# A graph-network kernel on one core: the last layer regrouped, its lists kept on chip, and buffer waits by bytes

## The chip, the cores and the metric

The kernel runs on one core of one Trainium2 chip. The metric is the device time of one execution in microseconds (us). Five executions of the kernel before took 2224.06, 2224.08, 2226.6, 2227.36 and 2230.5 us; the median is 2226.6 us.

The core has five engines that matter here, each with its own in-order queue: PE multiplies matrices, DVE does elementwise work, ACT does functions such as exp and also copies and casts, POOL does elementwise work and issues the indirect transfers (gathers and scatters whose row numbers lie in a tile), and SP issues the plain transfers. An instruction starts when those before it on its engine have started their turn and its semaphores have the values it waits for. So a wait holds up everything behind it on the same engine.

## The reference

The input x is 8 batches x 2048 nodes x 64 features, and adj is a 2048 x 2048 matrix of zeros and ones with ones on the diagonal. Four layers follow each other, each of the form x + layer(relu(layernorm(x))):

- layer 0: hypergraph attention over 64 hyperedges, mixed with the product of adj (rows divided by their degree) and the features;
- layer 1: a Chebyshev convolution with three terms, and a weight matrix for each node, made from 16 embeddings;
- layer 2: three steps of message passing with adj;
- layer 3: graph attention.

Layer 3 is the one that is changed most:

```python
h = jnp.einsum('bni,io->bno', x, weight)
e = leaky_relu((h @ a[:D, 0])[:, :, None] + (h @ a[D:, 0])[:, None, :], 0.2)
e = adj[None, :, :] * e
h_prime = jnp.einsum('bij,bjd->bid', softmax(e, axis=-1), h)
```

Where adj is 0 the score is 0 and not minus infinity. So a node's result is a weighted sum over its few neighbours plus one common weight times the sum of all other nodes' features.

## The kernel before

**Layout.** Most layers hold x as four pairs q of two batches, so 128 partitions are 2 batches x 64 features, in chunks of 512 nodes. The product with adj goes through 16 row tiles of adj (`adj_t`, loaded by SP, cast by ACT at L295, multiplied by PE into `pp`). Nodes are sorted by degree early on; `orders` holds the sorted order, 16 tiles of 128 nodes.

**Who sets the order.** The kernel is written with pools and tiles. A scheduler puts the instructions of each engine in an order of its own, so the order in the file is not the order of issue, and it adds the semaphore waits. A pool is released at the end of its `with` block. A tile of a later pool that lies on the same bytes waits; before the change it waits for all users of the released pool.

**Neighbour lists** (`neighbours`, L1468). While layer 2's first steps run on PE, DVE finds for each sorted tile t from 1 to 15 the node numbers of at most NEAR[t] neighbours of each of its 128 nodes (20, 14, 12, 10, 9, 8, 8, 7, 6, 6, 5, 5, 4, 4, 3, together 121). At its end two DVE instructions make row numbers and a mask of them, and SP stores both (128 x 242 numbers) to DRAM.

**The last layer.** `Scores` (L1880 on) computes for each tile of nodes the 512 features of h (8 batches x 64) and 16 scores, and stores them as rows of 528 numbers in DRAM (`f_rows`). Then `layer3_near` (L1520) builds a `Near` object and runs two generators side by side:

- `first_tile` (L2039) handles tile 0, the 128 nodes with the most neighbours, densely. It gathers their rows of adj, transposes them (`at`), and goes through 16 column tiles jt. For each, DVE copies the features to `h` (L2092), which has a column of ones; PE adds the plain product (`plain`). For each of 8 batches ACT computes two exps (L2099, L2100), DVE takes their maximum (L2101) and multiplies it by adj (L2102), 128x128 each, and PE adds the product with h (`first`). It yields after each batch.
- `others` (L1987) handles the tiles 1 to 15 in the order TILES, one block each. `block` (L1970) has POOL gather the tile's own rows and those of its neighbours from f_rows into a ring of 40 rows (`fetch`, L1953; the gathers show as L1955). Some ten small DVE instructions and two exps on ACT make the weights (L1999 to L2016). Then DVE multiplies each gathered row by its weights (`scaled`, L2034, 128x512) into one of four buffers, the sum of all rows last, and PE adds it through the identity matrix into `acc`. It yields after each row. A division gives `o`. The block after the next one is then gathered, and `put_back` (L1964) has POOL scatter the `o` of the block before to DRAM (`att_rows`, L1966).

Each yield of `others` lets `first_tile` take one step. When both are done, `result` (L2122) loads `att_rows` in 16 tiles of 256 KB (L2132) into three buffers, PE transposes them (L2135), DVE adds them to x (L2137; x is loaded a chunk at a time into two buffers, L2128), and SP stores each chunk in four pieces (L2141).

**Other lines that the prediction touches.** L1264 and L1268 load the convolution's weights, L1271 subtracts two of them, and `pk` are its products; L1228 are transposes for layer 1; L607 is the end of layer 0's mixing; L203 makes the low half of a split number (`ah_n_lo` among them).

## Time and profile before

| | |
|---|---|
| median of five executions | 2226.6 us |
| the profiled execution | 2230.18 us |
| its span from the first to the last instruction | 2228.5 us |
| mean granted TensorE clock | 0.904 |
| instructions | 21758 |
| TensorE busy | 1959.0 us (88%) |
| VectorE busy | 1136.8 us (51%) |
| POOL busy | 708.2 us (32%) |
| data moved | 254.03 MB |

The span divides into layer 0 (0 to 680 us), layer 1 (680 to 1397), layer 2 (1397 to 1934) and the last layer (1934 to 2228). In the page's slices each digit is the busy share of a fortieth of the span, 55.7 us. In lists of groups, a row has the line, the engine, the operation, the tiles written and read, and the count; then busy time in us and the mean duration of one in ns; then the idle time of the engine just before such instructions and what ended it. In timelines a row has start and duration in us, and in brackets the idle time before it. DVE instructions overlap: the next one starts some 0.08 us before the end of the one before, so the time from start to start is shorter than the duration. POOL's gathers show 0.95 us or more each, with 0.30 us of issue between them.

### The profile page before, as it was taken

The numbers are of one execution on the slowest core, as the hardware profiler recorded it, in microseconds if no ns is written. First come the engines' busy times: TensorE is split into PE (matmuls) and PEld (weight loads), VectorE is DVE, ScalarE is ACT, GpSimd is POOL, SyncE is SP. The second block draws the span as 40 slices with busy tenths as digits, with TensorE's granted clock in tenths as the row PEclk, the third lists the DMA queues.
The fourth block names the chain that finished last, engine by engine and source line by source line (L and its number), as shares of the span: only waits on it lengthen the run. The fifth ranks groups of instructions, "written<-read, shape, count | busy, mean of one in ns | idle before, by whom it ended". The sixth has DMA issues, their size and how long they took to land.

```text
span 2228.5 us, 21758 instructions
## 1 busy us (share of the span) xinstructions
PE 1959.0 (88%) x7530; PEld 1191.7 (53%) x7530; DVE 1136.8 (51%) x2292; ACT 711.0 (32%) x1331; POOL 708.2 (32%) x609
## 2 busy tenths in 40 slices
PE   5777899997879998999999998998999999679883
PEld 1454766662226775344353543776777677445442
DVE  7846667754663121533425344897402222359892
ACT  6402355544443442011020200422534333245430
POOL 0013066755330001735727266012000000177740
PEclk8857799997676998999999999899999999789895
DMA  8231123352103345022050400455434444377735
GB/s 319 69 100 28 44 92 106 125 157 85 38 38 107 125 106 163 0 94 58 23 128 0 114 1 22 171 189 197 155 113 133 133 152 143 124 198 199 205 107 201
DMA packets 108032, 254.03 MB, mean 114 GB/s; under 512 B 19632, under 2 KB 20032, under 8 KB 100608
## 3 DMA queue, kind: packets, MB, share of 16 engines
q1 hardware_dynamic: 90288, 185.46, 26.4%
q0 software_dynamic: 17616, 67.00, 10.1%
q8 instruction: 63, 1.03, 0.2%
q14 instruction: 65, 0.53, 0.1%
HBM read 218.49 MB, written 33.93 MB: 113 GB/s over the span
## 4 chain that ended last, share of the span: by engine, by line
PE 59%; DVE 10%; POOL 5%; DMA 5%; issue 4%; ACT 3%; SPq 1%; POOLq 0%; DVEq 0%; ACTq 0%
PE pp L136 24%; PE pk L136 16%; PE acc L136 5%; PE bank L136 4%; PE p L136 2%; POOL ring L1955 2%; PE pn L136 2%; DMA q<-in_adj_dram,order 2%; POOL dt L633 1%; POOL q L1794 1%; DMA adj_t<-in_adjT_dram 1%; PE pd L136 1%; DVE q L1809 1%; DMA q<-att_rows 1%; PE pt L1228 1%
## 5 line engine op out<-in xcount | busy, mean ns | idle before, releaser
L295 ACT CAST adj<-adj_t 128x512 fp32r<-128x512 f32 x384 | 237.0, 620 | 728.9 <-PE pp L136 622.2
L1354 POOL TENSOR_TENSOR acc<-acc,y 128x512 f32<-128x512 f32 x224 | 277.1, 1269 | 450.1 <-DVE y L1349 450.1
L136 PE MATMUL pk<-q,w 128*128 128x512 f32 (+1 forms) x1024 | 358.3, 612 | 14.1 <-DVE w L1271 11.9
L136 PEld LDWEIGHTS pk<-q,w 128*128 128x128 f32 (+1 forms) x1024 | 136.6, 188 | 232.1 <-issue 181.2
L1349 DVE SCALAR_TENSOR_TENSOR y<-pk,bias,q 128x512 f32<-128x512 f32 x224 | 157.7, 746 | 139.8 <-PE pk L136 133.4
L136 PE MATMUL acc<-q,ident 128*128 128x512 f32 x416 | 218.3, 627 | 11.4 <-ACT q L1829 6.2
L136 PE MATMUL pp<-adj,u_n_hi 128*128 128x512 f32 x768 | 213.1, 397 | 0.0
L136 PE MATMUL pp<-adj,u_n_lo 128*128 128x512 f32 x768 | 209.2, 392 | 0.0
L136 PEld LDWEIGHTS pp<-adj,u_n_hi 128*128 128x128 f32 x768 | 143.9, 188 | 34.8 <-issue 6.4
L136 PEld LDWEIGHTS pp<-adj,u_n_lo 128*128 128x128 f32 x768 | 144.6, 188 | 29.6
L1955 POOL DMA_INDIRECT ring<-f_rows,near x121 | 124.6, 1030 | 36.9 <-issue 17.1
L2048 POOL IOTA q<- 128x2048 int32 x1 | 1.8, 1834 | 348.9 <-PE p L136 348.9
L1794 POOL TENSOR_TENSOR q<-q,beta 128x512 f32<-128x512 f32 x57 | 67.5, 1184 | 111.0 <-DVE pick L1750 79.6
L136 PEld LDWEIGHTS acc<-q,ident 128*128 128x128 f32 x416 | 73.2, 197 | 52.5 <-issue 26.6
L1349 DVE SCALAR_TENSOR_TENSOR acc<-pk,bias,q 128x512 f32<-128x512 f32 x32 | 22.6, 747 | 146.8 <-PE pk L136 146.8
L136 PE MATMUL pp<-adj,x_ind_hi 128*128 128x512 f32 x256 | 95.0, 488 | 2.2 <-DVE q L701 1.8
L2034 DVE TENSOR_TENSOR q<-ring,e 128x512 f32<-128x512 f32 x136 | 91.2, 683 | 3.5 <-PE acc L136 3.3
L136 PEld LDWEIGHTS first<-h,m 128*128 128x128 f32 x256 | 47.6, 203 | 78.8 <-DVE m L2102 35.3
L136 PE MATMUL bank<-std,from_rows 32*128 32x512 f32 x128 | 47.1, 911 | 41.9 <-DVE std L243 33.8
L136 PE MATMUL pp<-adj,h_n_hi 128*128 128x512 f32 x256 | 77.6, 415 | 0.0
L136 PE MATMUL pp<-adj,h_n_lo 128*128 128x512 f32 x256 | 75.4, 407 | 0.0
L136 PE MATMUL pp<-adj,ah_n_hi 128*128 128x512 f32 x256 | 73.7, 408 | 0.0
(381 smaller groups left out, 3238.7 us busy)
## 6 DMA issues: line engine op xcount, KB each, us to landing
adj_t<-in_adjT_dram SPq DMA_DIRECT2D x160, 512.0 KB, 3.8
rows<-in_adj_dram SPq DMA_DIRECT2D x16, 1024.0 KB, 5.4
adj_t<-in_adjT_dram SPq DMA_DIRECT2D x64, 256.0 KB, 3.1
q<-x SPq DMA_DIRECT2D x12, 1024.0 KB, 4.8
q<-in_embT_dram SPq DMA_DIRECT2D x8, 1024.0 KB, 11.4
x<-q SPq DMA_DIRECT2D x8, 1024.0 KB, 3.9
x_ch<-in_xT_dram SPq DMA_DIRECT2D x4, 1024.0 KB, 6.2
h_rows<-q SPq DMA_DIRECT2D x16, 256.0 KB, 2.9
```

The source lines that it names most:

```text
L136: self.nc.tensor.matmul(out, lhsT, rhs, start=start, stop=stop)
L295: nc.scalar.copy(moving, at[:, i])
L633: nc.gpsimd.tensor_sub(dt, th[0], th[1])
L1228: nc.tensor.transpose(pt[:, q], src(q)[h, s], ident[h, h])
L1349: nc.vector.scalar_tensor_tensor(y, pks[b, half], bias[:, b : b + 1], emb[:, b], op0=OP.add, op1=OP.mult,)
L1354: nc.gpsimd.tensor_add(acc, acc, y)
L1794: self.nc.gpsimd.tensor_tensor(x, x, by.unsqueeze(2).to_broadcast([P, NB, D]), op=OP.mult)
L1809: nc.vector.tensor_add(d, d, self.pas.pop(i - 1))
L1955: self.nc.gpsimd.indirect_dma_start(to, None, self.kern.f_rows[:], bass.IndirectOffsetOnAxis(ap=index, axis=0))
L2034: self.nc.vector.tensor_tensor(to.rearrange(split, b=NB), src.rearrange(split, b=NB), by.unsqueeze(2).to_broadcast([P, NB, D]), op=OP.mult,)
L2048: nc.gpsimd.iota(whole, pattern=[[1, N]], base=0, channel_multiplier=0)
```

## The change

Six things change.

1. Every pool is opened with `reuse_waits="tile"`: a tile on released bytes waits only for the users of these bytes, and no longer for all users of the released pool.
2. The neighbour lists stay on chip, in a tile that lives through the whole kernel (`kern.near`). The two DVE instructions that make row numbers and mask of them move from the end of `neighbours` to the start of the last layer; store and load go.
3. The ring has 36 rows instead of 40. The exps of `first_tile` get a tile of their own on a slot (`self.m`, two sets for all 8 batches); `result` gets 16 buffers for `att_rows` instead of three.
4. The start: gathers of the first two blocks are issued first, then `first_tile` takes twelve steps, then both go on side by side.
5. `others` multiplies two gathered rows with one DVE instruction of 128x1024, the sum of all rows and the first row first; it yields after two rows.
6. In `first_tile` ACT copies the features to `h`, of which there are two with fixed ones; max and multiplication take all 8 batches of a column tile in one DVE instruction of 128x1024; it yields four times per column tile.

```diff
-            tc.tile_pool(name="att", bufs=1) as w,
+            tc.tile_pool(reuse_waits="tile", name="att", bufs=1) as w,
...
-        near = k.tile([P, FIRST[NT]], F, name="near")
+        near = self.near
...
-        both = k.tile([P, 2, FIRST[NT]], I32, name="near_both")
-        nc.vector.tensor_scalar(both[:, 0], near, 1.0, -1.0, op0=OP.max, op1=OP.add)
-        nc.vector.tensor_scalar(both[:, 1].bitcast(F), near, 0.0, None, op0=OP.is_gt)
-        nc.sync.dma_start(self.near, both)
...
             near = Near(self, slots, w, ps)
             first = near.first_tile()
+            others = near.others()
             next(first)
-            for part in near.others():
+            next(others)
+            for _ in range(12):
+                next(first)
+            for part in others:
                 next(first, None)
...
-    RING = 40
+    RING = 36
...
+        self.m = slots.tile([P, 4, NB, P], F, name="m", tag="q0")
+        self.att = Halves(slots, "att", ("q0", "q1"), True)
...
-        near = w.tile([P, 2, FIRST[NT]], I32, name="near")
-        nc.sync.dma_start(near, kern.near)
-        self.near, self.there = near[:, 0], near[:, 1].bitcast(F)
+        self.near = w.tile([P, FIRST[NT]], I32, name="near")
+        nc.vector.tensor_scalar(self.near, kern.near, 1.0, -1.0, op0=OP.max, op1=OP.add)
+        self.there = w.tile([P, FIRST[NT]], F, name="there")
+        nc.vector.tensor_scalar(self.there, kern.near, 0.0, None, op0=OP.is_gt)
...
         ready = [self.block(t) for t in self.TILES[:2]]
+        yield
...
-            for i in range(n + 1):
-                y = self.y[:, self.turn % 4]
-                self.turn += 1
-                by, src = (e[:, i], block[:, i, : NB * D]) if i < n else (none, self.total)
-                self.scaled(y, src, by)
-                kern.mm(acc, kern.ident, y, start=i == 0, stop=i == n)
+            for i in range(-1, n, 2):
+                y = self.y[:, self.turn % 4 : self.turn % 4 + 2]
+                self.turn += 2
+                if i < 0:
+                    self.scaled(y[:, 0], self.total, none)
+                    self.scaled(y[:, 1], block[:, 0, : NB * D], e[:, 0])
+                elif i + 1 < n:
+                    nc.vector.tensor_tensor(
+                        y.rearrange("n i (b f) -> n i b f", b=NB),
+                        block[:, i : i + 2, : NB * D].rearrange("n i (b f) -> n i b f", b=NB),
+                        e[:, i : i + 2].unsqueeze(3).to_broadcast([P, 2, NB, D]), op=OP.mult,
+                    )
+                else:
+                    self.scaled(y[:, 0], block[:, i, : NB * D], e[:, i])
+                for j in range(min(2, n - i)):
+                    kern.mm(acc, kern.ident, y[:, j], start=i + j < 0, stop=i + j == n - 1)
                 yield
...
+        hs = [w.tile([P, NB, D + 1], F, name=f"h{i}") for i in range(2)]
+        for h in hs:
+            nc.vector.memset(h[:, :, D:], 1.0)
         for jt in range(NT):
-            h = w.tile([P, NB, D + 1], F, name="h", bufs=3)
-            nc.vector.memset(h[:, :, D:], 1.0)
-            nc.vector.tensor_copy(
-                h[:, :, :D], self.rows(jt).rearrange("n (b f) -> n b f", b=NB)
-            )
+            h = hs[jt % 2]
+            nc.scalar.copy(h[:, :, :D], self.rows(jt).rearrange("n (b f) -> n b f", b=NB))
+            m, m2 = (self.m[:, 2 * (jt % 2) + i] for i in range(2))
+            for b in range(NB):
+                nc.scalar.activation(m[:, b], on_all[:, 0, b], AF.Exp, bias=ed[:, jt, b : b + 1])
+                nc.scalar.activation(m2[:, b], on_all[:, 1, b], AF.Exp, bias=ed2[:, jt, b : b + 1])
+                if b % 4 == 3:
+                    yield
+            nc.vector.tensor_max(m, m, m2)
+            nc.vector.tensor_mul(m, m, at[:, jt].unsqueeze(1).to_broadcast([P, NB, P]))
+            yield
             kern.mm(plain, at[:, jt], self.rows(jt), start=jt == 0, stop=jt == NT - 1)
             for b in range(NB):
-                m = w.tile([P, P], F, name="m", bufs=4)
-                m2 = w.tile([P, P], F, name="m2", bufs=4)
-                nc.scalar.activation(m, on_all[:, 0, b], AF.Exp, bias=ed[:, jt, b : b + 1])
-                nc.scalar.activation(m2, on_all[:, 1, b], AF.Exp, bias=ed2[:, jt, b : b + 1])
-                nc.vector.tensor_max(m, m, m2)
-                nc.vector.tensor_mul(m, m, at[:, jt])
                 kern.mm(
-                    accs[b // 4][:, b % 4, : D + 1], m, h[:, b],
+                    accs[b // 4][:, b % 4, : D + 1], m[:, b], h[:, b],
                     start=jt == 0 and b % 4 == 0, stop=jt == NT - 1 and b % 4 == 3,
                 )
-                yield
+            yield
...
-                r = self.parts[:, t % 3]
+                r = self.att(t)
                 nc.sync.dma_start(r, kern.att_rows[t * P : (t + 1) * P])
```

## The prediction

> **What bounds the kernel.** I read the page's totals first, then the slices, then the last layer by itself. PE is busy for most of the span, and most of the change lies in the last layer, from 1934 us to the end:
>
> ```profile
> PE 1959.0 (88%) x7530; PEld 1191.7 (53%) x7530; DVE 1136.8 (51%) x2292; ACT 711.0 (32%) x1331; POOL 708.2 (32%) x609
> ...
> PE   5777899997879998999999998998999999679883
> ...
> DVE  7846667754663121533425344897402222359892
> ...
> POOL 0013066755330001735727266012000000177740
> ```
>
> Up to slice 34 PE follows PE, so there only PE's idle time can be won. In the last layer (slices 35 to 40) three engines are near their limits at once. The table of 10 us windows shows it (columns: window, length, PE, PEld, DVE, ACT, POOL busy, granted clock, DMA share, GB/s):
>
> ```profile
> 1990.00:2000.00 10.00, 1.20 (x3) 0.93 (x4) 3.07 (x13) 1.06 (x4) 7.56 (x9) 0.62 0.96 223
> ...
> 2040.00:2050.00 10.00, 10.00 (x34) 5.18 (x33) 10.00 (x30) 4.60 (x13) 7.87 (x8) 1.00 0.67 188
> ...
> 2150.00:2160.00 10.00, 7.18 (x21) 3.26 (x20) 9.73 (x28) 0.47 (x2) 2.41 (x2) 1.00 0.14 52
> ```
>
> POOL's 7.87 is a full queue: each gather shows 0.95 us of work and 0.30 us of issue. From 1939.07 to 2138 it starts 148 transfers without a pause, and nothing can end before its last gather, which starts at 2135.98. DVE and PE then still have four blocks to do; the last `o` is ready at 2176.2. So in the layer's first part the gathers set the time (1990 to 2000: everyone waits for the block of 21 rows), in the second part DVE with PE. The groups of this layer, by shape:
>
> ```profile
> L1955 POOL DMA_INDIRECT ring<-f_rows,near x121 | 124.6, 1030 | 36.9 <-issue 17.1 <-DVE m L2102 4.9 <-DVE m L2101 4.9
> L2034 DVE TENSOR_TENSOR q<-ring,e 128x512 f32<-128x512 f32 x136 | 91.2, 683 | 3.5 <-PE acc L136 3.3
> ...
> L2101 DVE TENSOR_TENSOR m<-m,m 128x128 f32<-128x128 f32 x128 | 36.2, 288 | 3.4 <-ACT m L2099 3.3
> L2102 DVE TENSOR_TENSOR m<-m,q 128x128 f32<-128x128 f32 x128 | 36.1, 286 | 0.0
> ```
>
> **What a DVE instruction does to a gather.** The releasers of L1955 are DVE lines, though no gather depends on them. The timeline shows why:
>
> ```profile
> 1945.32 0.95 POOL L1955 DMA_INDIRECT ring<-f_rows,order  x1 [0.30 <-issue]
> 1945.41 2.35 DVE L2052 SCALAR_TENSOR_TENSOR q<-q,own 128x2048 f32<-128x2048 int32 x1 [7.38 <-DMA q<-in_adj_dram,order]
> 1946.57 2.00 POOL L1955 DMA_INDIRECT ring<-f_rows,near  x1 [0.30 <-issue]
> ```
>
> The third line starts 1.16 us into a long two-input DVE instruction and takes 2.00 us instead of 0.95: it waited until that instruction was nearly through. Of the 110 transfers that start between 1991 and 2138, those that start inside a 128x512 L2034 are longer by up to 0.45 us, about what is left of it; the mean start-to-start time is 1.336 us instead of 1.25. The wait is thus 0.085 us per transfer. Random arrival would give 65 us of L2034 in 147 us times half of 0.60 us, 0.13, plus 0.03 for the short ones; so about half of random was paid.
>
> **Part 1, DVE's work in the last layer.** Instructions back to back start every 0.20 us (128x128) and 0.60 us (128x512), so an element of a row costs 1.04 ns and an instruction 0.07 us. A 128x1024 then takes 1.14 us. The nearest two-input row, L1271 at 64x1024, lasts 1.22 us against 0.683 for 512: bounds 1.14 and 1.37 (twice 512); I take 1.14. Behind the block of 21 rows there are 13.5 of 16 column tiles of the first tile and 53 of 58 pairs. Max and mul: 13.5 x (16 x 0.20 - 2 x 1.14) = 12.4 us; the copies to h that go to ACT, 13.5 x 0.41 = 5.5; pairs, 53 x (1.20 - 1.14) = 3. Together 21 us of the 154 us that DVE is busy from 2000 to 2170. ACT gets 16 copies of about 0.57 us and is busy 3 to 7 of every 10 us, so they cost nothing; if it were full they would cost 9 us. PE keeps its work: a row's two matmuls take 0.86 us at full clock and a head's 0.22. From 1997 on that is about 148 us, which by itself would end at 2145. Near lists from chip: two DVE instructions replace a 121 KB load (2.1 us) that the first gather waited for. The load of order stays in SP's queue, so the first gather starts about 1 us earlier (0 to 2). The ring of 36 only makes the last block wait for rows read long before: nothing, and at most one block's 5 us.
>
> So DVE's backlog behind the last gather shrinks to nothing, and **the gathers become the bound**. In the order of the changed program the last row is the 149th transfer from the first ring gather (146th before, two more scatters stand ahead). Its start is 1990.6 + 110 x (1.25 + w), w being the wait per transfer. Behind it come its landing, 4.5 us (a gather of 2067.40 lets its block start at 2072.44), and 13 us: the last block's scores stand ahead of six rows of the block before, so twelve rows at 0.86 and about 2.5 us of first multiply and `o`.
>
> Now w. Long two-input instructions, 53 pairs and 27 max or mul of 1.14 us, fill 91 us of about 155; a random arrival in one waits 0.57, so 0.34 in the mean. The lower bound is the 0.085 of today. I take 0.22, two thirds of random, nearest to the share paid today. Last gather 2152.3, last `o` 2169.8 against 2176.2: **-6 us**. With 0.085 it would be -20 (PE would then need 93% to follow), with 0.34 +7.
>
> The Trainium skill (SBUF — State Buffer, section "Who interferes with whom") says that a DVE instruction with two SBUF inputs contends with a GpSimd instruction that reads SBUF, and that the second to issue blocks fully. That speaks against longer instructions here. Taken at its word, every arrival waits, and this part would be +7 and the whole -10; the trace, with half of random, stands for less.
>
> **Part 2, the tail.** The chain after the last scatter:
>
> ```profile
> 2176.52 2.71 DMA att_rows<-o,order
> 2179.25 2.65 DMA q<-att_rows
> ...
> 2189.70 4.64 DMA q<-att_rows
> ...
> 2198.72 4.51 DMA q<-att_rows
> ...
> 2208.03 5.32 DMA q<-att_rows
> ```
>
> With three buffers, each set of loads waits for transposes, and SP issues it behind the stores of the chunk before. From 2179.25 the stores of the four chunks start 8.6, 17.1, 26.9 and 38.1 us later. Changed: nine loads go out at once, 0.45 us apart; a tile takes PE and DVE 1.02 us. Chunk 0 is done at 7.7 and chunk 1 at 11.8. The load of x for chunk 2 waits for the landing of chunk 0's stores (4.1 us after the last issue) and takes 5.0: 18.8. Chunk 2 is done at 22.6; the last two loads stand behind its stores in SP's queue, 24.4, land 4.6 later; chunk 3's stores start at 30. **-8 us**; -3 if the transfers only share what is already 0.97 and 0.88 busy in 2190 to 2210, -12 if they do not slow each other.
>
> **Part 3, waits at the seams.** I followed each buffer wait to the instruction that it names after the change. Four move where PE is idle. At 262.20 the first adjacency loads waited for the last reader of the released pool; their own bytes were free 5 us earlier; ACT waited 2.78 us for the landing and PE 4.55 behind it: -3 (0 to -3.5). At 76.6 the second phase's first product: -2 (0 to -2.6). At 675.7 transposes behind the last DVE of the mixing: -1 (0 to -2). At 828 the weight loads of the convolution:
>
> ```profile
> PE pk L136 <- DVE w L1271: 11.9, 1, 11.9
> ...
> DVE w L1271 <- DMA w<-in_wk_dram: 6.3, 1, 6.3
> ```
>
> SP is free to issue them from about 821 instead of 828.17. DVE is not done with ah_n_lo until 837.5, so at most 7 of the 11.9 us go; but the DMA share is about 1.0 from 822 on, so the loads may only move in among embT's: -3 (0 to -7). The other moved waits lie upstream of busy PE. **-9 us** (0 to -15). Everything behind a seam follows PE, so what is won is kept.
>
> **Sum.** -6 -8 -9 = -23 us on the profiled execution, 2230.2 (span 2228.5 and 1.7 around it): 2207. That execution lies 3.6 us above the median of the five, so 2204 for the median.
>
> **Rivals.** (a) The gathers keep their pace, w about 0.1, because scores and stalls leave gaps between the long instructions as today: part 1 is -19, the whole -36, 2191. For it: half of random today; against it: DVE's longest instruction doubles. (b) The waits at the seams are replaced by full DMA queues; parts 1 and 2 remain: -14, 2213. For it: the DMA share at 822. (c) Slower: a gather falls in step with PE's pace of a pair of rows, 1.72 us instead of 1.25. Then w is 0.47 through the layer, the last gather 2180, `o` 2197.7, 21.5 us later than before; with the other parts 2231, and 2240 if the seams give nothing. It is slower from w = 0.43 on. For it: 1.14 us is nearly one gather's cycle of 1.25, so a gather just released meets the next long instruction at its start. Against: where gathers are late, DVE idles and blocks nobody. (d) No change: w near 0.34 and a third of the seams and tail: within 0.2%, which is about what can be told from no change here.
>
> **Chances.** Forecast band 2195 to 2209, with its neighbours to 2218: 50%; (a) 18%; (b) up to 2222: 12%; (d) 8%; (c) 12%. Faster by over 0.2%: 80%. The range leaves out the far ends of (a) and (c): 2186 to 2229.
>
> **What would show it.** In the changed profile: the mean of the ring gathers near 1.17 us instead of 1.03 (near 1.05 would be rival a, 1.4 rival c), more of them released by DVE multiplies; DVE's busy time in the last layer down by 25 to 45 us, by count of instructions' durations; the wait for near gone; the chunk stores of the tail 30 us after its start; PE's wait for w near 9 us. I would be wrong most of all if DVE and PE lose time to each other on two pair buffers and lumps of eight heads, so that the backlog behind the last gather stays.

## The result, and the profile after

The changed kernel takes 2225.45 us (median of 42 runs) against 2228.41 us of the kernel before (79 runs): a ratio of 0.9985, 95% interval 0.9976 to 0.9994. The forecast was 2204. Only about a seventh of the forecast gain came; in the number the result is rival (d), no change within 0.2%, but not by that rival's account (below). The profiled execution has a span of 2224.3 us against 2228.5, at the same granted clock of 0.904.

Three places give the account. They are read from the two traces: how much earlier the n-th of the 7530 matmuls starts ("PE's lead"), the first gather into the ring, the end of the last `o`, and the end.

| | before | after | difference |
|---|---|---|---|
| PE's lead in the middle of layer 2 (1506 us) | | | -13.7 |
| PE's lead at the end of layer 2 (1922 us) | | | -6.3 |
| last matmul of the scores to first ring gather | 6.0 | 4.8 | -1.2 |
| first ring gather to last ring gather | 195.7 | 217.0 | +21.3 |
| last ring gather to last `o` | 40.3 | 26.8 | -13.4 |
| last `o` to the end | 52.2 | 47.9 | -4.3 |

So PE was 13.7 us ahead in the middle of layer 2, of which 7.4 were lost again inside layer 2, where the code is the same; the last layer's main part became 8 us longer instead of 6 shorter; the tail gave half of what was forecast.

The page of the changed kernel, its totals and slices:

```profile
PE 1967.1 (88%) x7530; PEld 1188.6 (53%) x7530; DVE 1116.5 (50%) x1980; ACT 708.9 (32%) x1347; POOL 727.9 (33%) x609
...
PE   5877899987879979999999998998999999679873
...
DVE  7846767744762032434424254998302222349763
...
POOL 0012066755420002726537176011000000277760
```

DVE has 312 instructions fewer, POOL as many as before but 20 us more of busy time. Ten-microsecond windows of the changed kernel (columns as in the windows above: length, PE, PEld, DVE, ACT, POOL, granted clock, DMA share, GB/s):

```profile
2040.00:2050.00 10.00, 9.08 (x32) 4.74 (x32) 9.96 (x16) 8.07 (x27) 7.87 (x8) 1.00 0.67 194
2120.00:2130.00 10.00, 4.02 (x6) 1.79 (x7) 4.81 (x14) 0.47 (x2) 7.69 (x8) 0.66 0.66 208
2140.00:2150.00 10.00, 6.55 (x8) 2.72 (x9) 6.23 (x14) 0.47 (x2) 7.56 (x9) 0.66 0.72 209
2150.00:2160.00 10.00, 9.72 (x23) 4.09 (x22) 8.89 (x18) 0.43 (x2) 3.73 (x3) 1.00 0.32 110
```

At 2040 all is full, as before. At 2120 and 2140 POOL alone is full, PE and DVE are in part idle, and the granted clock is 0.66: there the gathers are the bound, as forecast. From 2150 on PE is full again (9.72 of 10 us), and behind the last gather it sets the time. The groups by shape show what they cost:

```profile
L1959 POOL DMA_INDIRECT ring<-f_rows,near x121 | 139.7, 1154 | 67.6 <-issue 57.3 <-DMA ring<-f_rows,near 2.4 <-DVE den L2020 2.3
L2030 DVE TENSOR_TENSOR q<-ring,e 128x1024 f32<-128x1024 f32 x58 | 70.0, 1219 | 10.6 <-PE acc L135 10.4
...
L2117 DVE TENSOR_TENSOR q<-q,q 128x1024 f32<-128x1024 f32 x16 | 19.6, 1224 | 0.1
```

1154 ns for a gather instead of 1030; forecast was 1.17 us. The waits (engine, what waits, for what: us in total, times, longest), first of the kernel before, where `e` is L1999, then of the changed kernel, where it is L2004:

```profile
DVE e L1999 <- DMA att_rows<-o,order: 10.7, 1, 10.7
...
DVE e L1999 <- DMA ring<-f_rows,order: 6.4, 1, 6.4
...
DVE e L1999 <- DMA ring<-f_rows,near: 6.0, 2, 4.9
```

```profile
DVE e L2004 <- DMA ring<-f_rows,near: 20.0, 4, 9.4
...
PE acc L135 <- DVE q L2049: 17.2, 4, 8.5
...
DVE e L2004 <- DMA att_rows<-o,order: 14.2, 1, 14.2
...
PE pk L135 <- DVE w L1270: 11.4, 1, 11.4
...
DVE e L2004 <- DMA ring<-f_rows,order: 7.8, 1, 7.8
```

The scores of the blocks (`e`) need rows that gathers bring, whichever transfer the profile names. DVE waited 23.1 us for them before, in four waits, and waits 42.0 now, in six, and PE waits behind it. The line of `pk` is the seam at the convolution's weights: 11.9 us before, 11.4 now, forecast 9.

### The profile page after: what moved, and what is told of

It reads as the page before. It is cut to its first block, busy times and chain, and to the rows that moved or that the text cites. A ratio compares the mean times of both kernels' runs of the same rounds, so it can differ in the third digit from the quotient of the medians.

```text
span 2224.3 us, 21410 instructions
## 1 busy us (share of the span) xinstructions
PE 1967.1 (88%) x7530; PEld 1188.6 (53%) x7530; DVE 1116.5 (50%) x1980; ACT 708.9 (32%) x1347; POOL 727.9 (33%) x609
## 4 chain that ended last, share of the span: by engine, by line
PE 59%; DVE 8%; POOL 7%; issue 5%; DMA 4%; ACT 3%; SPq 1%; POOLq 0%; DVEq 0%; ACTq 0%
PE pp L135 26%; PE pk L135 16%; PE bank L135 4%; POOL ring L1959 3%; PE acc L135 3%; PE p L135 2%; PE pn L135 2%; POOL dt L632 1%; DMA q<-in_adj_dram,order 1%; POOL q L1794 1%; DVE q L1809 1%; PE pd L135 1%; PE po L135 1%; PE pt L1227 1%; PE pw L135 1%
## 5 line engine op out<-in xcount | busy, mean ns | idle before, releaser
L135 PE MATMUL pk<-q,w 128*128 128x512 f32 (+1 forms) x1024 | 358.2, 612 | 12.6 <-DVE w L1270 11.4
L135 PE MATMUL acc<-q,ident 128*128 128x512 f32 x416 | 204.6, 618 | 29.7 <-DVE q L2049 17.2
L135 PE MATMUL pp<-adj,u_n_lo 128*128 128x512 f32 x768 | 214.1, 398 | 0.0
L1959 POOL DMA_INDIRECT ring<-f_rows,near x121 | 139.7, 1154 | 67.6 <-issue 57.3
L1794 POOL TENSOR_TENSOR q<-q,beta 128x512 f32<-128x512 f32 x57 | 67.5, 1186 | 104.9 <-DVE beta L1770 81.6
L2030 DVE TENSOR_TENSOR q<-ring,e 128x1024 f32<-128x1024 f32 x58 | 70.0, 1219 | 10.6 <-PE acc L135 10.4
L1416 DVE TENSOR_TENSOR q<-pn,later 128x512 f32<-128x512 f32 x32 | 21.5, 688 | 101.5 <-PE pn L135 101.4
```

The source lines that it names most:

```text
L135: self.nc.tensor.matmul(out, lhsT, rhs, start=start, stop=stop)
L1416: nc.vector.tensor_add(to, pn, later[:, 2].unsqueeze(1).to_broadcast(full))
L1794: self.nc.gpsimd.tensor_tensor(x, x, by.unsqueeze(2).to_broadcast([P, NB, D]), op=OP.mult)
L1959: self.nc.gpsimd.indirect_dma_start(to, None, self.kern.f_rows[:], bass.IndirectOffsetOnAxis(ap=index, axis=0))
L2030: nc.vector.tensor_tensor(y.rearrange("n i (b f) -> n i b f", b=NB), block[:, i : i + 2, : NB * D].rearrange("n i (b f) -> n i b f", b=NB) ...
```

## The experiments

All ratios are to the kernel before, run beside. Two kinds of chips took part, and this matters. In the first series and in the last (chip 1) the kernel before takes 2228 us; the chip of the first series is not on record, and its kind is taken from this time. On four other chips (10, 5, 9 and 8) it takes 2273 to 2276, with the first three layers as long as on the first kind and the last one some 50 us longer (one profile of the kernel before, before_again, shows this). Only numbers of one kind are compared. "Main" is the time from the first ring gather to the last `o`, "gather" the mean duration of a ring gather by near (L1959 in the changed kernel), "lead" PE's lead over the first profile of the kernel before at 1506 and at 1922 us. Two profiles of the kernel before differ in this lead by up to 7 us at 1400 and 3.8 us at 1922, so single leads are good to some 4 us.

| kernel | chips | us | ratio (95%) | lead | main | gather |
|---|---|---|---|---|---|---|
| before | first | 2228.4 | | 0, 0 | 235.9 | 1030 |
| after | first | 2225.5 | 0.9985 (0.9976 to 0.9994) | 13.7, 6.3 | 243.8 | 1154 |
| after_third | first | 2224.3 | 0.9986 (0.9968 to 1.0004) | 13.0, 6.9 | 241.0 | 1144 |
| hold | first | 2223.9 | 0.9971 (0.9954 to 0.9988) | 17.6, 15.9 | 243.6 | 1186 |
| best2 | first | 2210.6 | 0.9913 (0.9887 to 0.9938) | 13.3, 9.4 | 231.4 | 1083 |
| before_again | others | 2280.6 (one run) | | 3.2, 3.8 | 290.4 | 1017 |
| seams | others | 2261.5 | 0.9955 (0.9933 to 0.9977) | 13.0, 12.9 | 285.9 | 1027 |
| lists | others | 2248.9 | 0.9892 (0.9863 to 0.9921) | 11.7, 3.1 | 258.8 | 1133 |
| after_again | others | 2242.7 | 0.9868 (0.9840 to 0.9896) | 16.6, 8.4 | 256.5 | 1163 |
| aligned | others | 2237.0 | 0.9835 (0.9804 to 0.9866) | 14.7, 13.1 | 264.9 | 1152 |
| short_rows | others | 2240.0 | 0.9841 (0.9812 to 0.9870) | 17.8, 11.2 | 266.2 | 1063 |
| short_max | others | 2250.8 | 0.9918 (0.9888 to 0.9947) | | 268.7 | 1239 |
| short_both | others | 2259.1 | 0.9946 (0.9923 to 0.9969) | | 271.8 | 1241 |
| best1 | others | 2240.3 | 0.9849 (0.9820 to 0.9879) | 18.8, 14.9 | 253.0 | 1106 |
| late_e | others | 2240.0 | 0.9847 (0.9802 to 0.9891) | 21.1, 20.6 | 265.1 | 1192 |
| banks | others | 2236.8 | 0.9841 (0.9810 to 0.9872) | 15.1, 11.1 | 261.6 | 1181 |
| banks_y | others | 2237.1 | 0.9855 (0.9816 to 0.9893) | 17.9, 17.1 | 257.6 | 1150 |

### The two parts apart: seams, lists

```diff
# seams: the kernel before, with the new waits only (all 54 pools)
-        self.consts = ctx.enter_context(tc.tile_pool(name="consts", bufs=1))
+        self.consts = ctx.enter_context(tc.tile_pool(reuse_waits="tile", name="consts", bufs=1))
# lists: the changed kernel, with the old waits (the same lines the other way round)
```

> The kernel before, with the waits by bytes in every pool and nothing else. In the changed kernel PE was 10.4 us ahead of the kernel before from 679 us on and 13.3 us at 1520, and 6.3 us ahead at 1922. Theory: the waits win this much by themselves and the last layer is as before, so 6 to 10 us less than before, about 2220. Rival: what is won at the seams is lost in layer 2 for a reason that belongs to the waits; then PE's lead falls from about 13 us at 1520 to 6 at 1922 here too, each row tile of the product taking some 0.35 us longer, and the time is 2223 to 2226.

> The changed kernel with all pools opened as before (released buffers wait for the whole pool again); the last layer's five edits stay. Theory (the buffer waits gave about 13 us, the five edits lose: 6.6 in layer 2 through the moved tile, 7.9 between first gather and last o, and give back 4 behind it): about 10 us slower than the kernel before, 6 to 14. Rival (the five edits give what was forecast, 15 us, and the waits nothing): 10 to 15 us faster than before.

Seams is 11.7 us faster than the kernel before beside it (2261.5 against 2273.2, 5 to 15 by the interval). Its lead is 13.0 us in the middle of layer 2 and still 12.9 at its end: with the old last layer nothing of it is lost inside layer 2. Lists is not 10 us slower but 27 faster; its layers 0 to 2 end where those of the kernel before end on such a chip (lead 3.1 against 3.8), and all it wins is in the last layer, 258.8 us against 290.4. So on these chips the last layer's edits win what they do not win on the first kind. The expectation for lists was made from the first kind's traces and does not hold on another.

Lists also limits what the leads can show. Lists and the changed kernel beside it on the same chip (after_again) differ by the waits alone, and their times by 6.3 us. At 300 us the profiles with the new waits lead by 5.9 to 8.5 us, and lists and before_again by -0.1 and 0.1, so this much is the waits'. But at 1506 lists, with the old waits, leads by 11.7 too. So the waits are worth some 6 to 12 us, and not all of the 13.7 can be put down to them.

### The address of adj: aligned

In layer 2, 1536 matmuls `pp<-adj,u_n` stream adj tiles from SBUF. Moving `near` out of layer 2's pool shifted these tiles: by the sizes of the tiles ahead of them they lay at multiples of 64 bytes before, and 32 bytes past one after. The experiment adds 32 unused bytes ahead of them:

```diff
+            nc.gpsimd.memset(k.tile([P, 8], F, name="pad"), 0.0)
             w1v = self.block_diag(k, a["W1T"][:D], "w1v")
```

> The changed kernel with one unused tile of 32 bytes ahead of the others in the pool of layer 2; nothing else differs, so every adj tile of the 1536 products pp<-adj,u_n lies at a multiple of 64 bytes again, as in the kernel before (in the changed kernel they lie 32 bytes past one). Theory (the place of the streamed operand in SBUF sets the pace): start to start of these products 227 ns instead of 234, PE's lead over the kernel before stays near 13 us to the end of layer 2 instead of shrinking to 6, and the run is 6 to 7 us faster than the changed kernel. Rival (the slower pace comes from something that runs beside the products, or from another order on PE): still 234 ns, and no difference over 2 us.

The groups of these products, changed kernel, then aligned (the kernel before has 397 and 392 ns):

```profile
L135 PE MATMUL pp<-adj,u_n_hi 128*128 128x512 f32 x768 | 217.3, 402 | 0.0
L135 PE MATMUL pp<-adj,u_n_lo 128*128 128x512 f32 x768 | 214.1, 398 | 0.0
```

```profile
L135 PE MATMUL pp<-adj,u_n_hi 128*128 128x512 f32 x768 | 213.9, 398 | 0.0
L135 PE MATMUL pp<-adj,u_n_lo 128*128 128x512 f32 x768 | 210.9, 394 | 0.0
```

The pipelined matmuls start 227 ns apart (median) in the kernel before and in seams, 234 in all seven profiles of kernels with the shifted tiles, 229 in all seven with the pad. The lead shrinks by 7.4, 6.1 and 8.2 us from 1506 to 1922 in the three profiles of the changed kernel (6.1 to 8.6 in all seven with the shifted tiles) and by 1.6 in aligned (0.5 to 4.0 in all seven with the pad). Aligned is 5.7 us faster than the changed kernel on the same chip (2237.0 against 2242.7; the intervals of the ratios overlap, so the trace carries this more than the time). The shift of the tiles by 32 bytes is shown as the cause for most of the loss; 229 instead of 227, and a drift of 4 us in three other kernels with the pad, stay unexplained.

### DVE instructions beside gathers: short_rows, short_max, short_both, lock, best1

```diff
# short_rows: pairs of rows as two 128x512
-                    nc.vector.tensor_tensor(
-                        y.rearrange("n i (b f) -> n i b f", b=NB),
...
+                    for j in range(2):
+                        self.scaled(y[:, j], block[:, i + j, : NB * D], e[:, i + j])
# short_max: the first tile's max and product in 128x128
-            nc.vector.tensor_max(m, m, m2)
-            nc.vector.tensor_mul(m, m, at[:, jt].unsqueeze(1).to_broadcast([P, NB, P]))
+            for b in range(NB):
+                nc.vector.tensor_max(m[:, b], m[:, b], m2[:, b])
+                nc.vector.tensor_mul(m[:, b], m[:, b], at[:, jt])
# short_both: both; best1: short_rows, with pads for all 3072 products with adj
```

> The changed kernel with its pairs of rows multiplied by two 128x512 instructions again, all else as changed. In the changed kernel 110 transfers after the first scatter took 165.7 us, 1.507 each, against 1.336 before. Theory (a DVE instruction with two inputs from on chip memory holds up the gather that starts in it, until it ends): the ring gathers' mean falls from 1154 ns to about 1080, the last gather starts 8 to 10 us earlier, the time falls to 2215 to 2219. Rival (the order of the work, lumps of eight heads and pairs of buffers, makes the time): the last gather may move, the time stays within 3 us of 2225.

> The changed kernel with max and multiplication in 128x128 pieces again, eight of each for a column tile, one after the other. Theory: 32 of the 90 long instructions go, so the gathers' mean falls from 1154 ns to about 1110 and the last gather starts 4 to 6 us earlier; DVE gets 12 us more work, which its idle time takes: 2219 to 2224. Rival: DVE's 12 us show, 2228 to 2235.

> Both: rows in 128x512, max and multiplication in 128x128, the rest as changed. Theory: the gathers' mean is about the 1030 ns of before, the 110 transfers take about 148 us instead of 166, and the time falls by 10 to 15 us to 2210 to 2215, if DVE and PE follow. Rival: the time stays at 2222 to 2230, with DVE or PE late instead of the gathers.

> The changed kernel with 32 unused bytes in three pools, so that all 3072 products with adj tiles read them at multiples of 64 bytes (in the kernel before 1024 of them did not), and with each pair of rows multiplied as two 128x512 instead of one 128x1024. Theory: 6 to 7 us from layer 2's products, at most 7 more from the 1024 others (7 ns each, where PE sets the pace there), and in the last layer gathers of about 1.06 us instead of 1.15, up to 10 us less between first and last. So 8 to 24 us faster than the changed kernel. Rival (rows in two instructions cost DVE 58 starts more and gain nothing, since DVE's order sets the end): 6 us faster or less.

Rows of 512 bring the gather from 1163 (the changed kernel on such a chip) to 1063 ns, but main gets no shorter: 266.2 us against 256.5, with 27.0 us instead of 17.0 in which POOL stands between its transfers for more than the usual 0.30. Max and product in 128x128 make the gather longer than with 1024: 1239, against what the theory of "the longer the instruction, the longer the wait" said. The 21 gathers that start inside such a 128x128 take 1.44 us more than 0.95 in the mean, the longest 6.4 more. The gathers were then measured by themselves:

```python
# lock: per stage 24 gathers of 128 rows, beside a stream of one kind of DVE instruction
nc.vector.tensor_tensor(dst[:, k % 2, :n], src[:, :n], other[:, :n], op=OP.mult)
nc.gpsimd.indirect_dma_start(ring[:, k], None, table[:], bass.IndirectOffsetOnAxis(ap=here, axis=0))
```

> Only gathers and DVE instructions, nothing of the reference: eight stages of 24 gathers of 128 rows, beside a stream of DVE instructions. Theory (a DVE instruction that reads two operands from SBUF holds up the gather that POOL is writing, until that instruction ends): gathers 0.95 us beside nothing, beside copies (one operand) and beside products with one operand in PSUM; longer beside products of two SBUF operands, growing with their length: some 1.0 at 128x128, 1.3 at 128x512, 1.6 to 2.0 at 128x1024, 2.5 or more at 128x2048. Rival (any busy DVE costs the same): the three kinds of 512 and 1024 elements agree within 0.1 us.

POOL's timeline of this run (on chip 9, of the second kind), the first two gathers of four stages: beside a stream of products of 128x128, of 128x512, of 128x1024 and of 128x2048, all with two operands in SBUF.

```profile
50.02 0.95 POOL L100 DMA_INDIRECT ring<-table,idx  x1 [3.50 <-DVE dst L88]
51.27 84.17 POOL L100 DMA_INDIRECT ring<-table,idx  x1 [0.30 <-issue]
...
166.35 1.15 POOL L100 DMA_INDIRECT ring<-table,idx  x1 [3.41 <-DVE idx L84]
167.81 0.95 POOL L100 DMA_INDIRECT ring<-table,idx  x1 [0.30 <-issue]
...
246.06 1.68 POOL L100 DMA_INDIRECT ring<-table,idx  x1 [49.80 <-DVE idx L84]
248.05 1.97 POOL L100 DMA_INDIRECT ring<-table,idx  x1 [0.30 <-issue]
...
565.49 2.75 POOL L100 DMA_INDIRECT ring<-table,idx  x1 [49.93 <-DVE idx L84]
568.54 1.90 POOL L100 DMA_INDIRECT ring<-table,idx  x1 [0.30 <-issue]
```

| DVE stream (start to start) | mean gather, us |
|---|---|
| none | 0.951 |
| two SBUF operands, 128x128 (0.20) | one of 84.17, until the 418 instructions were over |
| two SBUF operands, 128x512 (0.60) | 0.954 |
| two SBUF operands, 128x1024 (1.135) | 1.954, the same with a broadcast operand |
| two SBUF operands, 128x2048 (2.20) | 1.933 |
| one operand in PSUM, 128x512 | 0.945 |
| copy, 128x1024 | 1.027 |

These means can't be read as the price of a length, because a steady stream and a steady row of gathers fall in step. What a gather waits for shows where it starts. The first gather of each stage starts 0.35 us into an instruction that has 0.33 us to go at 128x512, 0.87 at 128x1024 and 1.93 at 128x2048; it takes 0.20, 0.73 and 1.80 us longer than 0.95, which is what is left of the instruction less some 0.13. Behind it, at 128x1024 every gather starts 0.07 us into an instruction and waits nearly all of it; at 128x2048 1.2 us in, and waits for less than half of it. At 128x512 nearly all start together with an instruction and don't wait; the DVE instruction takes 0.72 us instead of 0.68. So the wait does grow with the length when starts are scattered, as they are in the kernels. In the kernel before, 63 transfers of the last layer start inside a 128x512 instruction of L2034 and take 0.20 us more in the mean; in the changed kernel 40 start inside a pair L2030 and take 0.50 us more, 39 of them by what is left of the pair less 0.13, within 0.06 us. Those that start together with an instruction wait for nothing. Together the transfers from the first ring gather to the last are longer than 0.95 us by 14.2 us before and by 28.7 after.

Short instructions without a gap between them are another matter: beside 128x128 one gather was shut out for as long as the stream lasted. This fits short_max and short_both, where 16 short instructions follow each other on a column tile.

The Trainium skill (SBUF — State Buffer, "Who interferes with whom") says that a DVE instruction with two SBUF inputs contends with a GpSimd instruction that reads SBUF, and that one with at most one SBUF input does not, outside the modes in which DVE uses a second port. The stages agree: with two inputs a gather that starts inside an instruction waits, and with one operand in PSUM all 24 take 0.94 to 0.95 us, wherever in an instruction they start.

Best1 is no faster than aligned on these chips (0.9849 and 0.9835), although its gathers are 46 ns shorter. What the shorter gathers are worth shows on the first kind of chip only, below.

### The order on DVE's queue: late_e

In the changed kernel the order on DVE's queue puts the scores of a block (`e`, L2004) ahead of rows of the blocks before. At 2116 it reads so:

```profile
2115.33 1.22 DVE L2030 TENSOR_TENSOR q<-ring,e 128x1024 f32<-128x1024 f32 x1
2116.47 0.28 DVE L2012 TENSOR_REDUCE top<-e 128x8 f32<-128x72 f32 x1
2124.58 0.24 DVE L2004 TENSOR_TENSOR e<-ring 128x80 f32<-128x80 f32 x1 [7.84 <-DMA ring<-f_rows,order]
2124.74 0.16 DVE L2013 TENSOR_SCALAR top<-top 128x8 f32<-128x8 f32 x1
```

The last gather of the block whose `top` is reduced at 2116.47 started at 2101. The rest of the work on its scores and its nine rows stand behind the scores of the next block (the third line), whose last gather starts at 2118; the wait ends at 2124.58. DVE waits 7.84 us with work at hand, and PE idles 7.22 us beside it.

```diff
-            e = w.tile([P, NEAR[1] + 1, NB], F, name="e", bufs=2)[:, :n]
+            e = w.tile([P, NEAR[1] + 1, NB], F, name="e", bufs=1)[:, :n]
```

> The kernel 'aligned' with one buffer instead of two for e, the weights of a block. The instructions that make a block's weights then stand behind all row products of the block before on DVE's queue; in the changed kernel they stand ahead of 2 to 10 of them, and since they wait for the block's last gather, PE runs dry with rows at hand. Theory: the gaps of PE of 5 to 8 us between 2060 and 2140 go, what is left behind the last gather falls from 20 to 27 us to some 17, and the run is 5 to 9 us faster than 'aligned' (ratio to before 0.980 where that one had 0.9835). Rival: with one buffer each block's weights (some 3 us on DVE and ACT) can't be made beside the rows of the block before, 15 times; where gathers set no pace that is up to 15 us slower.

The order became what was wanted (all rows of a block, then the scores of the next), and last gather to last `o` fell to 17.0 us from 25.6 in aligned. But the last gather came 9 us later after the first one (248.2 instead of 239.2), so main stayed at 265 and the ratio at 0.985. The gap behind the last gather can be closed; by this means it moves ahead of it. Neither theory is confirmed by the time.

### Why other chips differ: after_again, before_again, handoff, handoff2, banks, banks_y, hold

> The changed kernel itself, unaltered, so that it, its variants and the kernel before are timed side by side. On the first pair of runs its ratio was 0.9985. If the last layer's length depends on the chip (the kernel before took 2228 us in one series and 2273 us in another, with layers 0 to 2 alike), the ratio may differ where gathers wait for something else than DVE; if not, 0.997 to 1.0 again, with a first gather 6 to 8 us earlier than before and a stretch from first gather to last o 6 to 10 us longer.

> The kernel before, unaltered, profiled beside the other runs. Two later series gave it 2273 and 2276 us, where the first gave 2228; the changed kernel moved only from 2225 to 2243. Theory: the 45 us lie in the last layer alone (layers 0 to 2 end within 3 us of the first profile), as long stops in which ACT and DVE wait for a signal that PE should have given, while POOL issues gathers; the finer the steps, the more such stops. So its last layer takes about 280 us from first gather to last o instead of 236, with 30 us or more of such stops. Rival: the transfers themselves are slower there, so that the mean gather or its landing is longer by 20% or more.

The changed kernel gains 1.3% there. ACT and DVE stand still for long stretches in the last layer, which no trace of the first kind of chip shows. The waits of before_again, and two lines of the timeline of after_again ("remote": no signal in the profile explains the wait):

```profile
ACT m L2099 <- remote: 31.3, 8, 10.1
...
DVE q L2034 <- remote: 13.2, 2, 11.0
```

```profile
1977.32 0.59 ACT L2097 COPY q<-pt 128x512 f32<-128x512 f32 x1 [17.00 <-remote]
...
1985.80 0.69 DVE L2049 TENSOR_TENSOR q<-q,none 128x512 f32<-128x512 f32 x1 [26.67 <-remote]
```

By the program all of them wait for PE, whose matmuls had ended long before (at 1961.7 for the copy at 1977.32). The gathers themselves are not slower (1017 ns). Such waits add up to 50.8 us on ACT and DVE in before_again and to 73.7 in after_again. So their sum does not tell how much a kernel loses: main is 54.5 us longer there than on the first kind for the kernel before, and 12.7 for the changed one. Why the kernel before loses more, no run shows. To see the late signals alone:

```python
# handoff: 60 rounds on PE and ACT (or DVE), without and beside 40 gathers on POOL
nc.tensor.transpose(pt, x, ident)
nc.scalar.copy(x, pt)
```

> Only 60 rounds of a 128x128 transpose on PE and a copy of its result back (on ACT or on DVE), without and beside 40 gathers on POOL; nothing of the reference. Theory (where the last layer is long, PE's signal comes late while POOL issues gathers): a round of 0.8 to 1.2 us alone; beside gathers some rounds of 3 to 15 us, with the consumer waiting for PE. Rival (the stops come from something else in that layer, the order of the instructions or their loading): the rounds take the same time with and without gathers, within 0.2 us.

> Again only 60 rounds of a transpose on PE and a copy on ACT, nothing of the reference, beside five things: 40 gathers of 128 rows of 2112 bytes; 40 gathers of 128 rows of 528 bytes; 40 full gathers with some microseconds of POOL work between them; 40 plain loads of the same size issued by SP; and the first kind of gathers beside rounds of DVE and ACT without PE. In the run before, PE's signals were late only from the 22nd gather on, 28 us after the first, by 2.0 us mostly. Theory A (the bytes in flight hold the signal up): late beside full gathers and beside plain loads, not beside quarter rows or paced gathers. Theory B (the backlog of gather descriptors does): late beside full and quarter gathers, not beside loads. Either: if only PE's signal is concerned, the rounds of DVE and ACT keep their length (0.6 to 0.7 us); if every signal is, they are late too.

Without gathers a round takes 0.83 us and the copy starts 0.037 us after the matmul's end. Beside full gathers this holds for about 27 us; from the 22nd gather on nearly every signal is late, mostly by 2.0 us, to ACT and to DVE alike. ACT in handoff2, the last signal in time and the first three late ones:

```profile
46.66 0.27 ACT L89 COPY x<-pt 128x128 f32<-128x128 f32 x1 [0.57 <-PE pt L88]
47.82 0.27 ACT L89 COPY x<-pt 128x128 f32<-128x128 f32 x1 [0.90 <-PE pt L88]
50.63 0.27 ACT L89 COPY x<-pt 128x128 f32<-128x128 f32 x1 [2.54 <-issue]
53.42 0.27 ACT L89 COPY x<-pt 128x128 f32<-128x128 f32 x1 [2.52 <-issue]
```

Beside gathers with a quarter of the bytes the signals are late too, and stay late for 10 us after the last gather was issued; beside plain loads of the same size none is (0.037 us at most). In the stage of paced gathers the signals were late from 22 us on and no longer some 12 us after the gathers had slowed down, from one in 1.25 us to one in 2.09. The last 15 rounds of DVE and ACT without PE became longer as well (1.25 to 1.40 us, 0.59 to 0.67 before). So it is not the bytes, as theory A has it; a backlog that gathers leave (theory B) fits, though no run shows the backlog itself, and it is not PE's signal alone. What holds the signals up, and why the first kind of chip doesn't show it in this layer, is open; both runs were on chips of the second kind.

Three edits tried to avoid the exchange of signals there:

```diff
# banks (on aligned): two more PSUM banks, so PE need not wait for ACT
-                pt = ps.tile([P, 4, P], F, name="pt", bufs=2)
+                pt = accs[g] if i else ps.tile([P, 4, P], F, name="pt", bufs=2)
# banks_y (on banks): six row buffers
+        y = two.rearrange("p a q n -> p (a q) n")[:, 2:]
-                y = self.y[:, self.turn % 4 : self.turn % 4 + 2]
+                y = self.y[:, self.turn % 6 : self.turn % 6 + 2]
# hold (on banks_y): POOL waits after two blocks until the exchange is done
+                if place == 0:
+                    nc.gpsimd.tensor_copy(self.ring[:, self.at, :1], self.on_all[:, 1, NB - 1, :1])
```

> The kernel 'aligned' with one more edit: of the four groups of products that spread tile 0's scores (pt<-ident,ex), the last two go to the two PSUM banks that the products 'first' use later, instead of to the two pt banks again. PE then waits for no copy of ACT there. Theory (PE's signals come late while gathers run, and PE and ACT wait for each other in turn, three times in a row at this place): the three stops of ACT of 7.8, 17.0 and 7.6 us and DVE's stop of 26.7 us at the start of the last layer shrink to one of at most 17, and the run is 10 to 20 us faster than 'aligned' (ratio to before 0.975 to 0.979, where that one had 0.9835). On a chip without the late signals: within 2 us of 'aligned'. Rival (the stops have nothing to do with the exchange of signals): the same stops at another instruction, and no difference over 3 us.

> The kernel 'banks' with six buffers instead of four for the scaled rows (in two places that result no longer needs), so DVE may be three pairs ahead of PE instead of two. Theory (DVE waits for PE's late signals with all buffers full, and the order of the queue, made with the deeper buffers, has fewer rows behind a wait for gathers): 3 to 10 us faster than 'banks'. Rival (gathers alone set the pace from the middle of the layer on): within 2 us.

> The kernel 'banks_y' with one small POOL copy ahead of the third block's gathers, which needs tile 0's spread scores (on_all), so that POOL issues 9 gathers of the ring and then waits until PE and ACT have exchanged their signals at the start of the layer; before, it issues 43 in a row. Theory (signals come late only once some 20 gathers have been issued in a row): the stops of ACT of 8 and 15 us and that of DVE of 26 us at the start of the layer go, the first o ends about 15 us earlier after the first gather, and POOL waits some 10 us at the copy; since gathers set the pace later, most of that is lost again, so the run is 0 to 10 us faster than 'banks_y'. Rival (the stops are bound to those instructions, not to the backlog of gathers): they stay as long as they were, and the run is some 10 us slower by POOL's wait.

Banks and banks_y bring nothing in time. In banks ACT still stops 10.0, 17.6 and 4.1 us and DVE 27.1: with PE free to run on (its 32 products are through by 1952.1, and copies of them start on ACT as late as 1977.06 and 1982.02), the signal comes no earlier, so it is the signal, not the turn-taking, that is late. Hold came to the first kind of chip, where there are no such stops, so its question stays open; it shows something else there. It has the pad and the six buffers but products of 1024: gathers of 1186 ns and a main of 243.6 us, no better than the changed kernel.

### Back on the first kind of chip: best2, after_third

Best2 is short_rows with all pads, the two banks and the six row buffers.

> All products with adj at multiples of 64 bytes, rows in 128x512 again, the two more PSUM banks and six row buffers together. Theory: gathers of 1.06 us instead of 1.15 by the shorter instructions, and 6 us of layer 2; if gathers set the pace of the last layer, 5 to 10 us faster than 'banks_y' (ratio to before about 0.982). Rival (on this kind of chip the late signals set the pace, and shorter instructions exchange more of them): within 3 us of the changed kernel.

> The changed kernel unaltered once more, beside 'hold' and 'best2'. Ratio to before 0.985 to 0.989, as in the second series; if the series runs on a chip like the first one's (kernel before at 2228 us), 0.9985 and no stops by late signals, and then 'hold' should be slower than it and 'best2' 5 to 12 us faster.

The gathers by near of after_third, then of best2:

```profile
L1959 POOL DMA_INDIRECT ring<-f_rows,near x121 | 138.5, 1144 | 71.2 <-issue 58.0 <-DVE den L2020 5.0 <-DMA ring<-f_rows,near 3.0
```

```profile
L1963 POOL DMA_INDIRECT ring<-f_rows,near x121 | 131.0, 1083 | 70.3 <-issue 51.8 <-DMA ring<-f_rows,near 4.6 <-DVE den L2024 4.5
```

Best2 takes 2210.6 us: 13.7 less than the changed kernel, 17.6 less than the one before, and beats both. The profiled spans differ by 11.3 us, and 9.6 of these lie between first gather and last `o` (231.4 against 241.0), 8.4 of them before the last gather (211.1 against 219.5). Beside hold, which shares the pad, banks and six buffers, the gathers by near are 103 ns shorter (121 of them: 12.5 us) and main is 12.2 us shorter. By transfer, those from the first ring gather to the last are longer than 0.95 us by 28.9 us in after_third, 34.2 in hold and 21.4 in best2. Hold's wait on POOL and the wider pads differ too, so this is strong but not a clean single edit: the pairs of rows in 128x1024 are most of what the last layer lost by against the kernel before. On this kind of chip they were not taken out alone.

## Why the prediction was wrong, step by step

**The failed step is part 1** ("DVE's backlog behind the last gather shrinks to nothing ... last `o` 2169.8 against 2176.2: -6"). Counted from the first ring gather, it put the last gather at 212.0 and the last `o` at 229.5; measured are 217.0 and 243.8, in the repeat 219.5 and 241.0.

- The wait per transfer, w, was right: 0.22 us foreseen, 0.227 measured over the last 110 transfers (0.233 in the repeat), and 1.17 us foreseen for a ring gather, 1.154 measured. Its theory held too: a transfer that starts inside a pair waits for what is left of it (39 of 40 do so within 0.06 us), 0.50 us in the mean, where half of 1.14 is 0.57. The size of w was in part luck. It was picked between bounds as "two thirds of random"; the share paid before, half of random, would have given 0.17.
- What was not counted in the gathers is POOL's waiting for room in the ring: 3.0 us beyond the usual 0.30, at two gathers, and 5.4 in the repeat.

```profile
2000.74 1.76 POOL L1959 DMA_INDIRECT ring<-f_rows,near  x1 [2.32 <-DVE den L2020]
2003.81 1.04 POOL L1959 DMA_INDIRECT ring<-f_rows,near  x1 [1.31 <-DVE q L2116]
```

This is not the ring of 36 rows, for which the prediction allowed "at most one block's 5 us": by the program this block takes the same places with 40. The places were still in use, because the third block's rows were multiplied late, behind the scores of the block of 21 (its `o` ends at 2009.4, and at 1997.9 before). The rest of the 5 us lies in the first 38 transfers (51.3 us, where 50.3 was taken) and in w.

- "4.5 landing and 13 us" behind the last gather became 26.8, in the repeat 21.5. Blocks do start sooner after their last gather, 7 to 12 us from 2085 on, where it was some 25 to 31. But the step took DVE and PE for free to work off whatever had landed. The order of DVE's queue was in hand: scores stand ahead of rows that are ready, so PE idles (8.5 us at 2061, 7.2 at 2119, 5.3 at 2138, where the kernel before has one of 4.7 from 2000 on; another, of 12.5 at 1977, stood at 9.7 before), its clock falls to 0.66, and the rows left over come behind the last gather, where PE works almost without a break. The prediction counted this only for the last block ("the last block's scores stand ahead of six rows"). That the order does this is read from the trace. Late_e supports it: there the stretch behind the last gather fell to 17.0 us, about the 17.5 foreseen, but no time was won, and it ran on the other kind of chip.
- Rival (c), a gather in step with the long instructions, is what the stream of 128x1024 alone shows (one gather in 2.27 us). In the kernel the mean was 1.507, so there it did not happen. Rival (d) has the time but not the reason: w was 0.227, not 0.34, and the seams gave more than a third.

**A cost that the sum didn't have:** moving `near` shifts addresses in layer 2: +6 to 7 us. This is the second step that failed. The prediction costed the move by its instructions and its transfer alone, and called what is won at a seam "kept" because PE follows PE. The seams' gain was kept; 1536 matmuls behind became 7 ns slower each start to start in the median and 5.9 in the mean: 10.8 or 9.1 us by that product, 7.4 by the lead.

**Part 3, the seams, -9:** the leads are 13.7 and 13.0 us over the first profile of the kernel before and some 10 over the second; the time of seams says 11.7 and that of lists against the changed kernel 6.3. Right within what can be told. By place: 5.0 instead of 3 at 262. At the convolution's weights 0.5 us less wait instead of 3: the first load is issued at 810.42 instead of 828.17, 7.5 us more than PE's lead there, as foreseen; but the DMA share is 1.00 and 1.04 in the 20 us from 812 on, and DVE still waits 5.83 us for the loads instead of 6.25. That is rival (b), at this one seam.

**Part 2, the tail, -8:** -4.3. The stores and the loads of x in SP's queue:

```profile
2188.13 5.45 SPq L2159 DMA_DIRECT2D out_dram<-q  x8
2193.74 0.43 SPq L2146 DMA_DIRECT2D q<-x  x1
2194.22 1.83 SPq L2150 DMA_DIRECT2D q<-att_rows  x3
...
2205.15 1.80 SPq L2159 DMA_DIRECT2D out_dram<-q  x4
...
2213.36 2.09 SPq L2159 DMA_DIRECT2D out_dram<-q  x4
```

From the first load (2179.62) the chunks' stores start 8.5, about 12.2, 25.5 and 33.7 us later; foreseen were 7.7, 11.8, 22.6 and 30. The first half was right. In the second, the loads of `att_rows` come behind eight stores and beside the 1 MB loads of x, and the DMA share from 2194 to 2202 is 1.0. The load of x issued at 2193.74 lands 6.8 us later, where 5.0 had been taken, and the loads of `att_rows` issued at 2194.22 land 6.9 us later; DVE waits 8.93 us for them.

**The start, -1:** -1.2. **DVE's busy time** in the layer fell by 21.8 us (202.8 to 181.0 from the scores' last matmul on). By the sum of durations, for which 25 to 45 was foreseen, it fell by 50.6 (249.6 to 199.0), because DVE instructions overlap and there are far fewer of them; a 128x1024 takes 1.219 us, start to start 1.135, as taken.

**The sum:** foreseen -23. Found: -6.3 by the end of layer 2 (lead of 13.7 in its middle, 7.4 lost again), start and rounding -1.4, main +7.9, tail -4.3: -4.1, against a span shorter by 4.2. The sentence on what would make it wrong ("DVE and PE lose time to each other ... so that the backlog behind the last gather stays") named the right place, but had no term in the sum and no chance of its own. On the other chips the forecast -1% would have looked right (0.9868) for a reason that it did not contain.

## What to carry to other kernels

Before merging two-operand DVE instructions beside gathers, price the wait by what is left of an instruction when a gather starts in it: here 0.20 us in the mean inside a 128x512 and 0.50 inside a pair of 128x1024. Don't take the price from a steady stream alone, in which the two fall in step (none beside 128x512, twice the time beside 128x1024). When an engine stops being the bound, read the order of its queue again: instructions that wait for the new bound stand ahead of work that is ready, and what was hidden under a backlog becomes idle time. When a tile moves to another pool, look at the addresses of what it leaves behind.

## What the runs showed of the hardware that was not expected

- A matmul that streams 128x512 from SBUF started every 227 ns with the operand at a multiple of 64 bytes, every 234 at 32 bytes past one, and every 229 after a pad of 32 bytes (1536 matmuls in layer 2).
- A stream of 128x128 products with two SBUF operands, back to back, held one gather for 84 us, until it was over. In the same run a gather that started inside a product of 128x512, 128x1024 or 128x2048 took longer by what was left of it, less some 0.13 us (0.20, 0.73 and 1.80 us longer).
- On two chips, once some 20 gathers were issued without a pause, PE's signals reached ACT and DVE mostly 2.0 us late in the isolated runs. On these two and two more, ACT and DVE waited up to 29 us (28.8 in late_e) in the kernel's last layer for matmuls that had long ended; in no profile of the first kind of chip did they. The kernel before takes 290 us from first gather to last `o` there instead of 236, and the change is worth 1.3% there and 0.15% on the first kind.
